# Running sums and outer sums of an attention stage: from VectorE additions to accumulating transfers issued by GpSimd

## The chip, the cores and the metric

The kernel runs on one core of a Trainium2 chip. The metric is the device time of one execution in microseconds; the value compared is the median of three runs. All data are 32-bit floats. In this text TensorE is PE in the profile, VectorE is DVE, ScalarE is ACT, GpSimd is POOL, and SyncE (which only issues transfers) is SP.

## What is computed

Two layers follow each other on an input of shape (2, 512, 64, 64): two images of 4096 pixels with 512 channels. The first is a deformable convolution. The change touches only the second, which is self-attention over the pixels of each image, followed by a linear map and a normalization:

```python
px = jnp.transpose(x.reshape(B, C, N), (0, 2, 1))
q = jnp.tanh(px @ Wq.T)
k = jnp.tanh(px @ Wk.T)
v = px @ Wv.T
scores = jnp.einsum('bip,bjp,p->bij', q, k, align_w)
attn = jax.nn.softmax(scores, axis=2)
content = px + attn @ v
content = content @ Wfc.T + bfc
```

The softmax is computed without a maximum: exponentials of the scores are multiplied with the values, their sum over the keys is formed beside it, and the product is scaled by the reciprocal of that sum at the end.

## The kernel before

The span has three parts: the first layer (up to about 1216 us), and then for each of the two images a projection stage (keys, queries, values) and an attention stage, and at the end the normalization of the whole output.

In the attention stage the 4096 queries of an image are worked off in four **chunks** of 1024 queries, two halves (qh 0 and 1) of 512. The product of values and exponentials is done with a scheme of seven block products in place of eight (a Strassen-like one), and that twice, nested. At the outer level a chunk has seven passes p, each with one block combination of exponentials and one of values (`ORDER`); at the inner level `products` (L1467) does seven matmul groups of 128x128 by 128x256. A pass runs over eight groups of 512 keys (NG = 8) and a ninth that brings the residual in. Pass times group gives 63 **slots** to a chunk (`SLOTS`); slot l does pass l // 9, group l % 9.

For every key group there are four tiles of exponentials, each 128 x 1024: e0 and e1 (first half of the keys of the group, first and second half of the queries), e2 and e3 (second half of the keys). `produce` (L1389) makes one: two matmuls of scores into the single PSUM bank "st", then an exponential on ScalarE. `settle` (L1417) works on it one slot later. `EVENTS` (L1541) is the hand-written table that says in which slot l of its chunk each is made; negative slots lie in the last slots of the chunk before. The combinations for the outer level are formed in place ("outer sums", four of a group):

- `second_row` (L1410): e0 becomes e1 - e0, and e1 becomes e1 + e3 (L1413)
- `at`, L1588: e3 becomes e0 + e3, from slot 30 on, when the fourth pass is done with e3
- `at`, L1590: e2 becomes e2 - e3, from slot 40 on

`transform` (L1385) subtracts one quarter block from another in place, for the inner level. `inner_sums` (L1454) makes three more blocks (tile tt) from an exponential tile, four slots (LEAD) ahead of the products that use them.

The sums over the keys: `add_total` (L1403) adds a tile to the running total of its query half, 128 x 1024; e0 and e2 go to the total of half 0, e1 + e3 to that of half 1. `total` (L1426) adds the two halves of a total's columns; `spread_total` (L1432) sums over the partitions by a matmul with ones (tile pr) and copies the result to rin, which is used to scale the residual (`scale_residual`) and the outputs (`finish`).

All this is under a manual schedule: each engine runs its instructions in the order in which `slot` (L1592) writes them. The big tiles of the stage come from one pool, `ring`, 36 buffers of 4 KB a partition; a tile takes a buffer whose earlier tile has had its last use. The values of a slot (tile v, 448 KB) are loaded by SyncE three slots ahead, into four buffers. `load_queries` fetches the queries of the next chunk into a single buffer q. For the first chunk of an image the events with negative slots are done during the projection stage (`early_scores`, L1674), which leaves the rest of them to its end. GpSimd's only work in these stages is `sum_pixels` in the projections.

Of the kernel before, what the change touches and what calls it, by code (L numbers as in the profile page):

```python
# [10 lines left out]
F32 = mybir.dt.float32  # L11
I32 = mybir.dt.int32
AF = mybir.ActivationFunctionType
ALU = mybir.AluOpType
# [4 lines left out]
P = 128  # L19
# [508 lines left out]
NG = S // P // 4  # L528
# [6 lines left out]
def kernel(ctx: ExitStack, tc: tile.TileContext, t_in: dict, out: bass.AP):  # L535
# [7 lines left out]
    nc.vector.tensor_reduce(al[:, 1:2], al[:, 0:1], AX.X, ALU.max, apply_absolute_value=True)  # L543
    nc.vector.memset(al[:, 0:1], 1.0 / SCORE_MAX)
    window_path(tc, t_in, out, far, sums)


# [27 lines left out]
def window_path(ctx: ExitStack, tc: tile.TileContext, t_in: dict, out: bass.AP, far: bass.AP, sums: bass.AP):  # L575
    nc = tc.nc
# [66 lines left out]
    with ExitStack() as l0:  # L643
# [517 lines left out]
        with tc.manual_schedule():  # L1161
# [60 lines left out]
            for i in range(NSEQ):  # L1222
# [6 lines left out]
                w, m, g = Chain(weights, i + 1), Chain(sample, i), Chain(features, i + 3)  # L1229
# [12 lines left out]
    with ExitStack() as l1, tc.manual_schedule():  # L1242
        HC = C // 2
        HQ = CH // 2
        ring = l1.enter_context(tc.tile_pool(name="w1ring", bufs=36, reuse_waits="tile"))
        bnp = l1.enter_context(tc.tile_pool(name="w1bnp", bufs=1))
        bst = bnp.tile([P, KB, NB * NCH, 6], F32, name="bst")
        bfc = load("L1_conv_bfc", [P, KB], None, bnp)
# [3 lines left out]
        def piece(name, shape=(P, 2, CH)):  # L1252
            return ring.tile(list(shape), F32, tag="r", name=name)
# [15 lines left out]
        with ExitStack() as inner:  # L1269
            wk = inner.enter_context(tc.tile_pool(name="w1work", bufs=1))  # L1270
# [94 lines left out]
            def load_queries(n, k):  # L1365
                q = wk.tile([P, 2, CH], F32, name="q")
                for h in range(2):
                    nc.sync.dma_start(q[h * DQ : (h + 1) * DQ], q_d[n][k])
                return q
# [12 lines left out]
            def blocks(t):  # L1382
                return t.rearrange("p a (s q) -> p (a s) q", s=2)

            def transform(t):  # L1385
                x = blocks(t)
                nc.vector.tensor_sub(x[:, 1], x[:, 1], x[:, 0])
# [14 lines left out]

            def add_total(c, qh, t):  # L1403
                if qh in c.tot:
                    nc.vector.tensor_add(c.tot[qh], c.tot[qh], t)  # L1405
                else:
                    c.tot[qh] = piece("tot")
                    nc.vector.tensor_copy(c.tot[qh], t)

            def second_row(c, g):  # L1410
                t0, t1 = c.e["e0", g], c.e["e1", g]
                nc.vector.tensor_sub(t0, t1, t0)  # L1412
                nc.vector.tensor_add(t1, t1, c.e["e3", g])  # L1413
                if g < NG:
                    add_total(c, 1, t1)

            def settle(c, key, g):  # L1417

                e = c.e[key, g]
                if key in ("e0", "e2"):  # L1420
                    add_total(c, 0, e)
                transform(e)
                if key == "e1":
                    second_row(c, g)

            def total(c, qh):  # L1426
                t = c.tot[qh]
                nc.vector.tensor_add(t[:, 1, :], t[:, 1, :], t[:, 0, :])
                if qh:
                    nc.vector.tensor_add(t[:, 1, HQ:], t[:, 1, HQ:], t[:, 0, :HQ])  # L1430

            def spread_total(c, qh):  # L1432
                p = pair_bank("pr")[:, 0, :]
                nc.tensor.matmul(p, ones, c.tot.pop(qh)[:, 1, :], start=True, stop=True)
                nc.scalar.copy(rin[:, qh, :], p)

            def load_residual(c, qh):
                x = load_chunk(c.n, 2 * c.k + qh, nc.sync, "xq")
                for h in range(2):
                    c.e[f"e{2 * h + qh}", NG] = x[h]  # L1440

            def norm_residual(c, qh):
                for h in range(2):
                    normalize(c.e[f"e{2 * h + qh}", NG], 2 * h, *norms[c.n])

            def scale_residual(c, qh):
                for h in range(2):
                    t = c.e[f"e{2 * h + qh}", NG]
                    nc.vector.tensor_mul(t, t, rin[:, qh, :].unsqueeze(1).to_broadcast([P, 2, CH]))
                    transform(t)  # L1450
                if qh:
                    second_row(c, NG)
# [14 lines left out]
            def products(c, p, g, v, t):  # L1467
                if g == 0:
                    c.acc = bank("accx"), bank("accy")
                ax, ay = c.acc  # L1470
                x = blocks(c.e[ORDER[p][0], g])
                for out, blk, op, first, final in (
                    (ax[:, 0], 0, x[:, 0], True, False), (ax[:, 1], 2, x[:, 2], False, True),
                    (ax[:, 2], 4, t[:, 0], True, True),
                    (ay[:, 0], 3, t[:, 2], True, False), (ay[:, 1], 1, x[:, 1], False, True),
                    (ay[:, 2], 5, x[:, 3], True, False), (ay[:, 3], 6, t[:, 1], False, True),
                ):
                    nc.tensor.matmul(out, v[:, blk, :], op, start=(first and g == 0), stop=(final and g == NG))  # L1478

            def first_copy(c):  # L1480
                ax, ay = c.acc
                u = wk.tile([P, HQ], F32, name="u", bufs=2)
                nc.scalar.copy(u, ax[:, 0])  # L1483
                return u

# [53 lines left out]
                    yield from finish(c, t, 1, 0)  # L1539

            EVENTS = {}  # L1541
            for g, l in enumerate((-14, -13, -11, -10, -9, -7, -6, -5)):
                EVENTS.setdefault(l, []).append(("e0", g))
            for g in range(NG):
                EVENTS.setdefault(g - 4, []).append(("e2", g))
                EVENTS.setdefault(5 + g, []).append(("e3", g))
                EVENTS.setdefault(13 + g, []).append(("e1", g))

            class Attention:

# [5 lines left out]
                def before(self, l, c):  # L1556

                    for done in self.open:
                        settle(*done)
                    self.open = []  # L1560
                    for key, g in EVENTS.get(l, ()):
                        produce(c, key, g)
                        self.open.append((c, key, g))
# [10 lines left out]
                def at(self, l, c, s):  # L1574

                    if l in (-7, 8):
                        load_residual(c, int(l > 0))
                    if l in (-3, 11):
                        norm_residual(c, int(l > 0))
                    if l in (5, 22):  # L1580
                        spread_total(c, int(l > 5))
                        scale_residual(c, int(l > 5))
                    if l in (7, 25):
                        nc.vector.reciprocal(rin[:, int(l > 7), :], rin[:, int(l > 7), :])
                    if l in (6, 24):
                        self.sums(s + 2)
                    if 30 <= l < 31 + NG:
                        nc.vector.tensor_add(c.e["e3", l - 30], c.e["e0", l - 30], c.e["e3", l - 30])  # L1588
                    if 40 <= l < 41 + NG:
                        nc.vector.tensor_sub(c.e["e2", l - 40], c.e["e2", l - 40], c.e["e3", l - 40])  # L1590

                def slot(self, s):  # L1592
                    k, l = divmod(s, SLOTS)
                    c = self.chunks[k]
                    nxt = self.chunks[k + 1] if k + 1 < NCH // 2 else None
                    self.fetch(s + 3)
                    if l % (NG + 1) == 0 and self.ends:
                        next(self.ends[-1], None)
                    self.before(l, c)
                    if nxt and l >= 44:  # L1600
                        if l == 44:
                            nxt.q = load_queries(self.n, k + 1)
                        self.before(l - SLOTS, nxt)
                        self.at(l - SLOTS, nxt, s)
                    self.at(l, c, s)
                    if l + LEAD not in (8, 26):
                        self.sums(s + LEAD)
                    if l in (4, 21):
                        total(c, int(l > 4))
                    p, g = divmod(l, NG + 1)  # L1610
                    products(c, p, g, self.v.pop(s), self.t.pop(s))
                    for e in self.ends[:-1] if g == 0 else self.ends:
                        next(e, None)
                    if g == NG:
                        self.ends = self.ends[-1:] + [collect(c, p, first_copy(c), c.acc)]
# [50 lines left out]
            for n in range(NB):  # L1666
# [1 line left out]
                first = at.chunks[0]  # L1668
                pending = []
                early_events = deque(  # L1670
                    (l, key, g) for l in range(-16, 0) for key, g in EVENTS.get(l, ())
                )

                def early_scores():  # L1674
# [76 lines left out]
                for done in at.open:  # L1751
                    settle(*done)
# [5 lines left out]
                for s in range(NCH // 2 * SLOTS):  # L1758
                    at.slot(s)
                    l = s - (NCH // 2 - 1) * SLOTS  # L1760
# [88 lines left out]
```

## Time and profile before

| what | us |
|---|---|
| median of three runs (lowest to highest) | 3673.21 (3672.21 to 3676.82) |
| the profiled execution | 3674.86 |
| its span, first to last instruction | 3673.1 |
| TensorE busy | 3239.0 |
| VectorE busy | 2969.6 |
| ScalarE busy | 1362.9 |
| GpSimd busy | 272.5 |

The page divides the span into 40 slices and gives the busy share of each engine in tenths, the TensorE clock that was granted, and the busy share of the DMA engines. The attention stages are roughly slices 16 to 26 and 29 to 38, counted from 0:

```profile
PE   5789999999998867899899898998889989899890
DVE  8899999999995577877887878778787787877864
DMA  6334334334232454344353443555434344344379
```

What the reader sees: TensorE is nearly full in the attention stages, VectorE three quarters full, the DMA engines under half. An average over a stage doesn't tell which engine is waited for; that is read from the waits and the timeline.

### The profile page before, as it was taken

How to read it: one execution, taken by the hardware profiler on the slowest of the kernel's cores; microseconds unless marked ns; L12 is line 12 of the kernel's file. 1: busy time of each engine (PE TensorE's matmuls, PEld its weight loads, DVE VectorE, ACT ScalarE, POOL GpSimd, SP SyncE). 2: the span in 40 equal slices, each digit the busy share in tenths (PEclk: the TensorE clock that was granted, in tenths of full speed). 3: DMA queues.
4: the chain of work that ended last, by engine and by line, in shares of the span. 5: the costliest groups of instructions: out<-in, count | busy, mean ns of one | idle time of the engine just before them, and what ended most of it. 6: DMA issues, size and time to landing. Idle time of an engine off the chain costs nothing.

```text
span 3673.1 us, 37956 instructions
## 1 busy us (share of the span) xinstructions
PE 3239.0 (88%) x14147; PEld 2261.1 (62%) x14147; DVE 2969.6 (81%) x4107; ACT 1362.9 (37%) x1802; POOL 272.5 (7%) x186
## 2 busy tenths in 40 slices
PE   5789999999998867899899898998889989899890
PEld 2355555555555645686676776876577676686670
DVE  8899999999995577877887878778787787877864
ACT  2577778778775312203112022022202202203105
POOL 1121121121120110000000000011000000000000
PEclk9889999999999978999999999999899999999995
DMA  6334334334232454344353443555434344344379
GB/s 211 97 116 139 120 100 127 109 108 131 94 105 102 163 198 160 117 147 151 116 160 123 135 151 108 185 175 202 156 121 154 123 142 139 113 151 146 113 299 349
DMA packets 201634, 537.67 MB, mean 146 GB/s; under 512 B 25024, under 2 KB 26816, under 8 KB 200416
## 3 DMA queue, kind: packets, MB, share of 16 engines
q1 hardware_dynamic: 193920, 514.18, 41.9%
q10 hardware_dynamic: 7488, 20.97, 1.7%
q8 instruction: 113, 1.85, 0.2%
q14 instruction: 81, 0.66, 0.1%
q0 software_dynamic: 32, 0.00, 0.0%
HBM read 410.15 MB, written 124.91 MB: 146 GB/s over the span
## 4 chain that ended last, share of the span: by engine, by line
PE 63%; DVE 27%; DMA 4%; ACT 3%; issue 1%; POOL 1%; SPq 0%; ACTq 0%; DVEq 0%; POOLq 0%
PE accy L1478 20%; PE accx L1478 16%; DVE conv L820 9%; PE py L1004 6%; PE pS L1396 5%; PE pq L789 5%; PE pa L984 5%; DVE tot L1405 2%; DVE e L1412 2%; DVE e L1413 2%; PE pvy L1633 2%; PE pk L1700 1%; DVE tt L1458 1%; DVE vform L1332 1%; PE pvx L1633 1%
## 5 line engine op out<-in xcount | busy, mean ns | idle before, releaser
L1478 PE MATMUL accy<-tt,v 128*128 128x256 f32 x2016 | 602.2, 380 | 0.0
L1400 ACT ACTIVATE e<-pS 128x1024 f32<-128x1024 f32 x256 | 261.8, 1023 | 895.0 <-PE pS L1396 785.6
L1478 PE MATMUL accx<-e,v 128*128 128x256 f32 x1792 | 489.1, 396 | 25.8 <-DMA v<-wv 15.3
L1478 PEld LDWEIGHTS accx<-e,v 128*128 128x128 f32 x1792 | 329.5, 193 | 226.4 <-issue 153.1
L1478 PE MATMUL accy<-e,v 128*128 128x256 f32 x1792 | 461.7, 380 | 0.0
L820 DVE SCALAR_TENSOR_TENSOR conv<-xn,L_conv_dw_w_sb,conv 128x504 f32<-128x504 f32 (+1 forms) x512 | 409.4, 808 | 36.6 <-ACT conv L814 22.7
L1478 PEld LDWEIGHTS accy<-tt,v 128*128 128x128 f32 x2016 | 385.0, 191 | 53.0
L1478 PEld LDWEIGHTS accy<-e,v 128*128 128x128 f32 x1792 | 342.5, 191 | 47.3
L1396 PE MATMUL pS<-q,keys 64*128 64x512 f32 x1024 | 294.7, 653 | 35.1 <-ACT e L1400 25.5
L1458 DVE TENSOR_TENSOR tt<-tt,e 128x512 f32<-128x512 f32 x448 | 310.0, 692 | 15.3
L1478 PE MATMUL accx<-tt,v 128*128 128x256 f32 x1008 | 302.8, 382 | 0.0
L1457 DVE TENSOR_TENSOR tt<-e 128x256 f32<-128x256 f32 x448 | 187.6, 419 | 140.9 <-PE accy L1478 139.8
L984 PEld LDWEIGHTS pa<-bt,patch 96*128 96x128 f32 x2048 | 249.6, 196 | 57.1 <-issue 35.1
L984 PE MATMUL pa<-bt,patch 96*128 96x128 f32 x2048 | 253.1, 280 | 7.0 <-ACT bt L970 5.6
L970 ACT COPY bt<-pb 96x1024 f32<-96x1024 f32 x124 | 234.8, 2009 | 57.8 <-PE pb L965 53.9
L1483 ACT COPY u<-accx 128x256 f32<-128x256 f32 x56 | 20.9, 373 | 619.5 <-PE accx L1478 619.5
L789 PE MATMUL pq<-in_w,xn 128*128 128x512 f32 x512 | 239.3, 611 | 7.1 <-DVE o L882 5.0
L1004 PE MATMUL py<-dT,L_conv_out_w_sb 128*128 128x512 f32 x512 | 237.6, 609 | 4.7 <-ACT dT L995 4.7
L1405 DVE TENSOR_TENSOR tot<-tot,e 128x1024 f32<-128x1024 f32 x176 | 214.9, 1221 | 29.1 <-ACT e L1400 27.1
L1478 PEld LDWEIGHTS accx<-tt,v 128*128 128x128 f32 x1008 | 193.8, 192 | 27.1
L877 PE MATMUL po<-om_w_pg,feat 128*128 128x432 f32 x512 | 202.9, 540 | 3.0 <-ACT feat L860 3.0
L995 ACT COPY dT<-pa 32x256 f32<-32x256 f32 x496 | 179.6, 362 | 66.3 <-PE pa L984 57.0
(215 smaller groups left out, 4316.2 us busy)
## 6 DMA issues: line engine op xcount, KB each, us to landing
v<-wv SPq DMA_DIRECT2D x448, 448.0 KB
wv<-vform SPq DMA_DIRECT2D x112, 448.0 KB
patch<-xt SPq DMA_DIRECT2D x256, 192.0 KB
v<-ww SPq DMA_DIRECT2D x56, 448.0 KB
xt<-xj SPq DMA_DIRECT2D x128, 128.0 KB
res<-in_x SPq DMA_DIRECT2D x64, 256.0 KB
wx<-res SPq DMA_DIRECT2D x64, 256.0 KB
xq<-wx SPq DMA_DIRECT2D x32, 512.0 KB
```

The lines of the kernel that those rows point to most:

```text
L789: nc.tensor.matmul(pq, xn[:, kb, 1 + 2 * t : 3 + 2 * t, :].rearrange("p r c -> p (r c)"), in_w[:, kb, :], start=(kb == 0), stop=(kb == KB ...
L820: nc.vector.scalar_tensor_tensor(dst, src, wt, dst, ALU.mult, ALU.add)
L877: nc.tensor.matmul(po[:, : 3 * GP], f[:, kb, t * P : (t + 1) * P], om_w[:, kb].rearrange("p a k g -> p (a k g)"), start=(kb == 0), stop=(k ...
L970: copy(bt[:SN].rearrange("s g q d -> s d (g q)")[:, d0 : d0 + 4, :], pb[:SN])
L984: nc.tensor.matmul(pa[:, p], xp[:SN, p, cb * P : (cb + 1) * P], bt[:SN, 4 * cb : 4 * cb + 4, PX * s + p, :], start=True, stop=True,)
L1004: nc.tensor.matmul(py, out_w[:, kb, cb * P : (cb + 1) * P], dT[:, kb, :], start=(kb == 0), stop=(kb == KB - 1))
L1396: nc.tensor.matmul(p[:, a, :], keys[r, i, (2 * u + h) * P : (2 * u + h + 1) * P], c.q[r, qh, :], start=True, stop=True)
L1400: nc.scalar.activation(e.rearrange("p a q -> p (a q)"), p.rearrange("p a q -> p (a q)"), AF.Exp)
L1405: nc.vector.tensor_add(c.tot[qh], c.tot[qh], t)
L1457: nc.vector.tensor_sub(t[:, 0], x[:, 1], x[:, 3])
L1458: nc.vector.tensor_add(t[:, 1:3], t[:, 0].unsqueeze(1).to_broadcast([P, 2, HQ]), x[:, 0:3:2])
L1478: nc.tensor.matmul(out, v[:, blk, :], op, start=(first and g == 0), stop=(final and g == NG))
```

## The change

`add_total`, the addition of e3 in `second_row` and the addition at L1588 are no longer VectorE instructions but transfers from one SBUF tile to another that add to their destination, issued by GpSimd; the ninth group of `second_row` (the residual) stays on VectorE. The first tile of a total is still copied by VectorE. In `settle` the transform now stands ahead of the addition to the total, so what is added to total 0 is the transformed tile, and `total` undoes this for both halves with one more addition. Events are moved: e0 to slots -18 to -11, e2 to -9 to -2, e3 to 0 to 7 and e1 to 9 to 18 with two gaps (before: -14 to -5, -4 to 3, 5 to 12, 13 to 20). `total` of half 1 moves from slot 21 to 22, its `spread_total` from 22 to 23, the sum at L1588 from 30 to 29, the load of the next queries from slot 44 to 43. The ring has 38 buffers, u one in place of two.

```diff
@@ -1242,7 +1242,7 @@
     with ExitStack() as l1, tc.manual_schedule():
         HC = C // 2
         HQ = CH // 2
-        ring = l1.enter_context(tc.tile_pool(name="w1ring", bufs=36, reuse_waits="tile"))
+        ring = l1.enter_context(tc.tile_pool(name="w1ring", bufs=38, reuse_waits="tile"))
         bnp = l1.enter_context(tc.tile_pool(name="w1bnp", bufs=1))
         bst = bnp.tile([P, KB, NB * NCH, 6], F32, name="bst")
         bfc = load("L1_conv_bfc", [P, KB], None, bnp)
@@ -1402,7 +1402,7 @@
 
             def add_total(c, qh, t):
                 if qh in c.tot:
-                    nc.vector.tensor_add(c.tot[qh], c.tot[qh], t)
+                    nc.gpsimd.dma_start(c.tot[qh], t, accum_op=ALU.add)
                 else:
                     c.tot[qh] = piece("tot")
                     nc.vector.tensor_copy(c.tot[qh], t)
@@ -1410,24 +1410,25 @@
             def second_row(c, g):
                 t0, t1 = c.e["e0", g], c.e["e1", g]
                 nc.vector.tensor_sub(t0, t1, t0)
-                nc.vector.tensor_add(t1, t1, c.e["e3", g])
                 if g < NG:
+                    nc.gpsimd.dma_start(t1, c.e["e3", g], accum_op=ALU.add)
                     add_total(c, 1, t1)
+                else:
+                    nc.vector.tensor_add(t1, t1, c.e["e3", g])
 
             def settle(c, key, g):
 
                 e = c.e[key, g]
+                transform(e)
                 if key in ("e0", "e2"):
                     add_total(c, 0, e)
-                transform(e)
                 if key == "e1":
                     second_row(c, g)
 
             def total(c, qh):
                 t = c.tot[qh]
                 nc.vector.tensor_add(t[:, 1, :], t[:, 1, :], t[:, 0, :])
-                if qh:
-                    nc.vector.tensor_add(t[:, 1, HQ:], t[:, 1, HQ:], t[:, 0, :HQ])
+                nc.vector.tensor_add(t[:, 1, HQ:], t[:, 1, HQ:], t[:, 0, :HQ])
 
             def spread_total(c, qh):
                 p = pair_bank("pr")[:, 0, :]
@@ -1479,7 +1480,7 @@
 
             def first_copy(c):
                 ax, ay = c.acc
-                u = wk.tile([P, HQ], F32, name="u", bufs=2)
+                u = wk.tile([P, HQ], F32, name="u")
                 nc.scalar.copy(u, ax[:, 0])
                 return u
 
@@ -1539,12 +1540,11 @@
                     yield from finish(c, t, 1, 0)
 
             EVENTS = {}
-            for g, l in enumerate((-14, -13, -11, -10, -9, -7, -6, -5)):
-                EVENTS.setdefault(l, []).append(("e0", g))
-            for g in range(NG):
-                EVENTS.setdefault(g - 4, []).append(("e2", g))
-                EVENTS.setdefault(5 + g, []).append(("e3", g))
-                EVENTS.setdefault(13 + g, []).append(("e1", g))
+            for g, l in enumerate((9, 10, 12, 13, 14, 16, 17, 18)):
+                EVENTS.setdefault(g - 18, []).append(("e0", g))
+                EVENTS.setdefault(g - 9, []).append(("e2", g))
+                EVENTS.setdefault(g, []).append(("e3", g))
+                EVENTS.setdefault(l, []).append(("e1", g))
 
             class Attention:
 
@@ -1577,15 +1577,15 @@
                         load_residual(c, int(l > 0))
                     if l in (-3, 11):
                         norm_residual(c, int(l > 0))
-                    if l in (5, 22):
+                    if l in (5, 23):
                         spread_total(c, int(l > 5))
                         scale_residual(c, int(l > 5))
                     if l in (7, 25):
                         nc.vector.reciprocal(rin[:, int(l > 7), :], rin[:, int(l > 7), :])
                     if l in (6, 24):
                         self.sums(s + 2)
-                    if 30 <= l < 31 + NG:
-                        nc.vector.tensor_add(c.e["e3", l - 30], c.e["e0", l - 30], c.e["e3", l - 30])
+                    if 29 <= l < 30 + NG:
+                        nc.gpsimd.dma_start(c.e["e3", l - 29], c.e["e0", l - 29], accum_op=ALU.add)
                     if 40 <= l < 41 + NG:
                         nc.vector.tensor_sub(c.e["e2", l - 40], c.e["e2", l - 40], c.e["e3", l - 40])
 
@@ -1597,15 +1597,15 @@
                     if l % (NG + 1) == 0 and self.ends:
                         next(self.ends[-1], None)
                     self.before(l, c)
-                    if nxt and l >= 44:
-                        if l == 44:
+                    if nxt and l >= 43:
+                        if l == 43:
                             nxt.q = load_queries(self.n, k + 1)
                         self.before(l - SLOTS, nxt)
                         self.at(l - SLOTS, nxt, s)
                     self.at(l, c, s)
                     if l + LEAD not in (8, 26):
                         self.sums(s + LEAD)
-                    if l in (4, 21):
+                    if l in (4, 22):
                         total(c, int(l > 4))
                     p, g = divmod(l, NG + 1)
                     products(c, p, g, self.v.pop(s), self.t.pop(s))
@@ -1668,7 +1668,7 @@
                 first = at.chunks[0]
                 pending = []
                 early_events = deque(
-                    (l, key, g) for l in range(-16, 0) for key, g in EVENTS.get(l, ())
+                    (l, key, g) for l in range(-18, 0) for key, g in EVENTS.get(l, ())
                 )
 
                 def early_scores():
```

## The prediction

> **What bounds the kernel now.** I read the table of windows first, over one chunk of the attention stage (63 slots; some 247 us from the pr sum of one chunk to that of the next), then the waits of TensorE, then the rows of the VectorE instructions that the change touches, then the timeline of the slots in which TensorE stands still. Columns of the windows: busy time (count) of each engine, granted clock, DMA share, GB/s.
>
> ```profile
> 1953.00:2041.00 88.00, 75.10 (x311) 50.47 (x310) 69.25 (x95) 21.85 (x25) 0.00 (x0) 0.95 0.37 121
> 2041.00:2200.00 159.00, 159.00 (x705) 125.47 (x704) 129.99 (x184) 25.41 (x32) 0.00 (x0) 1.00 0.46 145
> ```
>
> In the second part of the chunk TensorE is busy all the time; in the first it is idle for 12.9 us of 88. So a chunk can give at most about 13 us, eight of them 103 us, whatever is taken off VectorE. The waits of TensorE over the whole run say where:
>
> ```profile
> PE pr L1434 <- DVE tot L1430: 82.5, 8, 10.3
> PE pS L1396 <- ACT e L1400: 25.5, 28, 1.2
> PE accx L1478 <- DMA v<-wv: 15.3, 5, 13.1
> PE accx L1478 <- DVE tt L1457: 10.5, 1, 10.5
> ```
>
> Eight waits of 10.3 us, one a chunk: the sum over keys of the second query half (pr) waits for its running total. The timeline shows why VectorE is late there:
>
> ```profile
> 2033.43 1.23 DVE L1412 TENSOR_TENSOR e<-e 128x1024 f32<-128x1024 f32 x1
> 2034.69 1.23 DVE L1413 TENSOR_TENSOR e<-e 128x1024 f32<-128x1024 f32 x1
> 2035.95 1.23 DVE L1405 TENSOR_TENSOR tot<-tot,e 128x1024 f32<-128x1024 f32 x1
> ...
> 2038.15 0.69 DVE L1428 TENSOR_TENSOR tot<-tot 128x512 f32<-128x512 f32 x1
> 2038.87 0.42 DVE L1430 TENSOR_TENSOR tot<-tot 128x256 f32<-128x256 f32 x1
> ...
> 2039.44 2.05 PE L1434 MATMUL pr<-tot,ones_k 128*128 128x512 f32 x2 [10.32 <-DVE tot L1430]
> ```
>
> In the eight slots that make e1, VectorE does 0.42+0.69 (inner sums) +0.42 (transform) +3x1.23 = 5.2 us where TensorE needs 4.28 us (3.02 in a slot without scores):
>
> ```profile
> 1982.71 1.13 PE L1478 MATMUL accx<-e,v 128*128 128x256 f32 x4
> ...
> 1986.99 1.13 PE L1478 MATMUL accx<-e,v 128*128 128x256 f32 x4
> ```
>
> It falls behind by 0.9 us a slot and by what else comes (collecting, scaling), until pr waits.
>
> ```profile
> L1405 DVE TENSOR_TENSOR tot<-tot,e 128x1024 f32<-128x1024 f32 x176 | 214.9, 1221 | 29.1 <-ACT e L1400 27.1
> L1413 DVE TENSOR_TENSOR e<-e 128x1024 f32<-128x1024 f32 x64 | 78.4, 1225 | 2.2
> L1588 DVE TENSOR_TENSOR e<-e 128x1024 f32<-128x1024 f32 x64 | 77.9, 1218 | 0.0
> al_f<-in_L_conv_align_w POOLq DMA_DIRECT2D x1, 0.2 KB, 6.9
> ```
>
> The last line is the only transfer that GpSimd issues before: 6.9 us to landing at the kernel's start, 0.66 us on GpSimd by its row. No accumulating transfer is in this trace.
>
> **What the Trainium skill says.** "DMA: Bandwidth & Descriptors", section on the anatomy of a GpSimd-issued DMA, fits 2.0 us plus bytes at 436 GB/s and says most of the 2 us is the write receipt, heaviest for HBM; no run here shows it. The same page, in its rules, says an accumulating DMA reads its destination and writes it later, so a second one on the same bytes has to wait for the first's semaphore: each addition to one total is a full round trip. "Collectives: The Full Stack", section on the bandwidth ceiling, says the add needs two source reads and so halves the rate. Nothing here confirms either.
>
> **The change part by part.** Removed from VectorE: 176 total adds x 1.22, 64 L1413 adds x 1.225, 64+8 L1588 adds x 1.22: 215+78+88 = 381 us; added 8 x 0.42 in total(). VectorE is not the bound outside the e1 slots, so this is worth only the stalls above. An e1 slot costs VectorE 2.8 us after it, under 4.28.
>
> Added: 312 transfers of 512 KB, 39 a chunk. Price of one, D: with one read counted 0.66+2.0+1.2 = 3.9 us, with two 0.66+2.0+2.4 = 5.1 us. I take 4.5: source and destination are both SBUF, where the receipt should be short, but loads share the engines.
>
> First total (e0, e2): 15 additions in a chain, first score in slot -18, total needed in slot 4, sum in slot 5. From the second event to there lie about 17 slots of 4.28 and three of 3.02, some 82 us, plus a little lead: 15 x 4.5 = 68 fits, 15 x 5.1 = 77 fits, from about 5.8 us on it is late. This is why the scores' four slots count.
>
> Second total: for each e1, transfer A adds e3 to it, transfer B adds it to the total, and B must wait for A. GpSimd is in order, so the next group's A is queued behind B's wait; nothing but such transfers is behind it there. The cycle c is A's trip with B's bytes in front of it on the same queue: 5.1 us at one read (0.66+2.0+2x1.2), 7.5 at two; I take 6.0. Slots after the change: scores in 9, 10, 12, 13, 14, 16, 17, 18, without one in 11 and 15 (3.02 us). From the start of slot 9, A can start (2.4 us for score and exponential, 0.42 and 1.23 on VectorE) at 4.1, 8.4, 15.7, 20.0, 24.3, 31.6, 35.8, 40.1. With D 4.5 and c 6.0 the ends of A from the third on are 20.2, 26.2, 32.2, 38.2, 44.2, 50.2; the last B ends at 54.7, total() adds 1.15: 55.9. pr now stands in slot 23, which starts at 52.4 (8x4.28+2x3.02 to slot 19, four of 3.02). Wait 3.5 us where it was 10.3: -6.8 x 8 = -54 us. The inner sums of the last e1 need A's end at 50.2 and TensorE its slot 25 at 58.4: covered.
>
> Waits of scores for the exponential in the same slots (two of 0.7 us a chunk, from buffers VectorE frees late) go: -1.5 x 8 = -12. Next late is the residual: spread one slot later leaves VectorE three slots, not four, for two multiplications, two transforms and two row sums (about 9 us with the copy of rin, against 9.1+1.8): I charge 1 us a chunk, +8.
>
> e3 += e0 (slots 29 to 37): one independent transfer every 3.02 us with three slots to the inner sums and four more to TensorE; hidden at D below some 15 us, if the engines keep up. The first addition of the second total is a copy on VectorE that waits for A (4.5 us); inner sums run four slots ahead, so it is covered.
>
> Queries are loaded in slot 43 and first used in 45, not 44 and 49: 6 us for 256 KB on SP behind one load of v. Hidden; if not, 1 to 3 us a chunk. Two more ring buffers and one less u: the e1 of group 7 is now made before an e1 is freed, so the two buffers keep the exponential from waiting; one u is free nine slots before its next use. Nothing.
>
> First chunk of each image: four more scores (2.25 us each, one bank) at the end of the projections. They fall into a gap (TensorE waits 13.1 us for the first v) and leave four slots 1.26 us shorter; but the last forms on VectorE, which that v waits for, come later in the queue. VectorE also drops 11 adds there (13 us). I set nothing, within 10 us either way an image.
>
> Sum against the profiled execution (3674.86 us, 1.8 around its span): -54-12+8 = -58, 3617. It lies 1.65 above the median of 3673.21: 3615.
>
> **The rivals.** One read, D 3.9, c 5.1: last B at 49.6, total at 50.7, no wait: -82-12+8 = -86, 3587. For: TensorE at 100% wherever VectorE is not late. Against: loads already take 37 to 46% of the DMA engines.
>
> Two reads with everything serial, D 5.1, c 7.5: A ends at 20.8, then 28.3 ... 58.3, B 63.4, total 64.5, wait 12.1, so +14-12+8 = +10: 3683 or, with a few us in the first chunks, no change.
>
> The DMA engines become the bound (slower). 145 GB/s at share 0.46 means some 315 GB/s for all sixteen; 39 x 0.52 MB x 2 reads in 247 us is 165 GB/s more, share 0.98. Then D grows past 5.8 and the first total's chain is late at slot 5: at 6.5, 15 x 0.7 = 10 us; c 8 makes pr wait 17.4 instead of 10.3, 7 us: +17 x 8 -12+8 = +132, 3805; at 6.0, some 3 and 3 us, 3717. It decides from D 5.8 on. For: the share; against: it counts the time packets took, and 348 GB/s were moved at 0.92 in the last stage.
>
> That VectorE isn't relieved can't be: the order of instructions has 312 adds fewer on it.
>
> **How the numbers follow.** Forecast 0.34; no wait at pr 0.23; two reads, serial 0.12; engines bound 0.31. The serial case is the one near zero: 0.07 within 0.2% (7 us, about what a measurement of this kernel can tell), the rest of it slower. Faster 0.57, same 0.07, slower 0.36. Likeliest case's own range: 3595 to 3650. Whole range: 3565 (no wait, and the first chunks gain 10 each) to 3790 (engines at D 6.4), leaving 0.05 below and 0.14 above.
>
> **What would show it.** Right: pr's wait on the total at 2 to 6 us, eight times; DVE near 2590 us; DMA share in the chunk's first half 0.6 to 0.8; accumulating transfers landing in 4 to 5 us. Wrong: a wait of TensorE or VectorE on tot in slot 4 or 5 (first total late), transfers landing in 6 us or more, new waits for v or q, or PE idle in the 3.02 us slots.

## The result, and the profile after

| | us |
|---|---|
| before, median of three | 3673.21 |
| after, median of three (lowest to highest) | 3921.08 (3919.97 to 3932.52) |
| after, profiled execution and its span | 3932.52, 3930.7 |

The ratio of after to before is 1.0682, 95% interval 1.0649 to 1.0714: slower by 6.8%. The change did what it says: VectorE's busy time fell from 2969.6 to 2607.7 us. TensorE waits more all the same. Its waits over the whole run after the change (engine, line, what it waited for: us in total, times, longest):

```profile
PE pr L1435 <- DVE tot L1431: 282.8, 16, 26.1
PE accx L1479 <- DMA v<-wv: 30.3, 36, 8.4
PE pS L1396 <- ACT e L1400: 22.7, 20, 1.2
PE accy L1479 <- DVE ct L1509: 18.1, 15, 3.6
```

Before, pr waited eight times, for the second total of each chunk. Now it waits sixteen times, for both totals of each chunk, and over three times as long in sum, +200 us: 87 us for the eight first totals (7.3 to 16.1 each) and 196 us for the eight second ones (21.5 to 26.1 each). The other rows add 15 us (v late) and 18 us (a PSUM bank not yet emptied, see below). VectorE isn't the cause but stands in between, as its own waits between 1500 and 2600 us show:

```profile
DVE tt L1458 <- DMA e<-e: 123.4, 23, 8.6
DVE tot L1430 <- DMA tot<-e: 58.0, 7, 19.1
DVE tot L1408 <- DMA e<-e: 22.9, 4, 6.4
```

L1430 is total(), L1458 the inner sums: VectorE, which is done early, waits for transfers to land. The issues of the transfers (KB each, median us from issue to landing) and the busy time by stretch of one chunk (second row: from the first pr sum to the second; third: after it):

```profile
tot<-e POOLq DMA_DIRECT2D x176, 512.0 KB, 5.3
e<-e POOLq DMA_DIRECT2D x128, 512.0 KB, 8.2
```

```profile
1940.00:2044.00 104.00, 90.54 (x378) 61.30 (x377) 47.91 (x83) 28.20 (x33) 12.89 (x15) 0.93 0.78 199
2044.00:2142.00 98.00, 71.45 (x297) 52.24 (x296) 49.55 (x76) 16.01 (x20) 13.05 (x15) 0.85 0.73 181
2142.00:2187.00 45.00, 43.68 (x201) 38.08 (x200) 31.63 (x48) 0.74 (x2) 7.74 (x9) 0.99 0.76 200
```

VectorE is half idle (49.55 of 98), TensorE is idle for 26.6 us of the same stretch, and the DMA engines went from shares of 0.37 to 0.46 to 0.73 to 0.78. GpSimd's own timeline in that chunk shows the two rhythms. First the chain of the first total, then the pairs of the e1 slots (L1414 is the outer sum, L1405 the addition to the total):

```profile
1997.63 0.86 POOL L1405 DMA_DIRECT2D tot<-e  x1 [6.31 <-DMA tot<-e]
2003.98 0.86 POOL L1405 DMA_DIRECT2D tot<-e  x1 [5.49 <-DVE tt L1459]
2009.82 0.86 POOL L1405 DMA_DIRECT2D tot<-e  x1 [4.98 <-DMA tot<-e]
...
2035.92 0.86 POOL L1405 DMA_DIRECT2D tot<-e  x1 [4.04 <-DMA tot<-e]
...
2088.66 0.86 POOL L1405 DMA_DIRECT2D tot<-e  x1 [7.74 <-DVE tt L1458]
2089.19 1.21 POOL L1414 DMA_DIRECT2D e<-e  x1
2097.62 0.86 POOL L1405 DMA_DIRECT2D tot<-e  x1 [7.21 <-DMA e<-e]
2098.15 1.21 POOL L1414 DMA_DIRECT2D e<-e  x1
2106.73 0.86 POOL L1405 DMA_DIRECT2D tot<-e  x1 [7.37 <-DVE tt L1458]
```

The six links from 1997.63 to 2035.92 take 6.4 us each, where a score comes every 4.28; pairs come every 9.0 us, where the slots give 5.04. (The mean link of a whole chunk is 6.3 to 6.9 us, the first chunk of each image apart. Where the bracket names VectorE in the pairs, VectorE had itself been released by the landing that the pair waited for; at 2003.98 its instruction only ended at about the same time.) Both totals are late for that reason.

A stall also costs after its end. TensorE's timeline around one (start, duration, matmuls):

```profile
2041.64 2.05 PE L1435 MATMUL pr<-tot,ones_k 128*128 128x512 f32 x2 [13.46 <-DVE tot L1431]
2043.47 1.91 PE L1479 MATMUL accx<-e,v 128*128 128x256 f32 x4
2045.18 1.06 PE L1479 MATMUL accx<-tt,v 128*128 128x256 f32 x2
2046.04 1.06 PE L1479 MATMUL accy<-tt,v 128*128 128x256 f32 x2
...
2049.50 1.13 PE L1479 MATMUL accx<-e,v 128*128 128x256 f32 x4
2050.47 0.59 PE L1479 MATMUL accx<-tt,v 128*128 128x256 f32 x2
```

The same groups take 1.91 and 1.06 us right after the stall and 1.13 and 0.59 us a slot later. TensorE's busy time grew from 3239.0 to 3285.9 us with the same 14147 matmuls. So +191 (pr, both kinds of wait on it: 282.8 against 82.5 + 9.0), +15 (v), +18 (PSUM), -10 (one wait for tt, gone) and +47 (slower matmuls) make 261; the spans differ by 258. The 47 us aren't all behind these stalls: part of them may lie in slots that wait for v, as the run with the sum of the fourth pass alone shows below.

### The profile page after: what moved, and what is told of

The parts are those of the page before. It is cut to its first block, busy times and chain, and to the rows that moved or that the text cites. A ratio compares the mean times of both kernels' runs of the same rounds, so it can differ in the third digit from the quotient of the medians.

```text
span 3930.7 us, 38681 instructions
## 1 busy us (share of the span) xinstructions
PE 3285.9 (84%) x14147; PEld 2277.6 (58%) x14147; DVE 2607.7 (66%) x3803; ACT 1363.1 (35%) x1802; POOL 542.3 (14%) x498
## 3 DMA queue, kind: packets, MB, share of 16 engines
q0 software_dynamic: 44960, 163.60, 22.1%
## 5 line engine op out<-in xcount | busy, mean ns | idle before, releaser
L1458 DVE TENSOR_TENSOR tt<-e 128x256 f32<-128x256 f32 x448 | 188.1, 420 | 555.6 <-PE accy L1479 300.9
L1479 PE MATMUL accx<-e,v 128*128 128x256 f32 x1792 | 502.2, 404 | 30.4 <-DMA v<-wv 30.3
L1405 POOL DMA_DIRECT2D tot<-e x176 | 151.4, 860 | 1315.3 <-DVE e L1387 409.0
L1396 PE MATMUL pS<-q,keys 64*128 64x512 f32 x1024 | 305.3, 668 | 31.6 <-ACT e L1400 22.7
L1459 DVE TENSOR_TENSOR tt<-tt,e 128x512 f32<-128x512 f32 x448 | 309.9, 692 | 15.3
L1435 PE MATMUL pr<-tot,ones_k 128*128 128x512 f32 x32 | 32.7, 1127 | 282.8 <-DVE tot L1431 282.8
```

Of the source, the lines that this page charges most:

```text
L1396: nc.tensor.matmul(p[:, a, :], keys[r, i, (2 * u + h) * P : (2 * u + h + 1) * P], c.q[r, qh, :], start=True, stop=True)
L1405: nc.gpsimd.dma_start(c.tot[qh], t, accum_op=ALU.add)
L1458: nc.vector.tensor_sub(t[:, 0], x[:, 1], x[:, 3])
L1459: nc.vector.tensor_add(t[:, 1:3], t[:, 0].unsqueeze(1).to_broadcast([P, 2, HQ]), x[:, 0:3:2])
```

## The experiments

Two theories. **Theory 1**: a transfer is a round trip, the additions to one total are a chain of them, and in the e1 slots GpSimd's order makes one cycle out of two. **Theory 2**: the bytes of loads and additions together fill the DMA engines. Each kernel below is the changed one with the edit shown; the last four start from the first one, the schedule alone. Diffs are cut to the lines that matter. Without an interval, the time is that of a single execution or two; before was at 3673.2 to 3676.9 us in these sessions.

**The schedule alone.** All additions go back to VectorE; the new slots stay.

```diff
-                    nc.gpsimd.dma_start(c.tot[qh], t, accum_op=ALU.add)
+                    nc.vector.tensor_add(c.tot[qh], c.tot[qh], t)
-                    nc.gpsimd.dma_start(t1, c.e["e3", g], accum_op=ALU.add)
+                    nc.vector.tensor_add(t1, t1, c.e["e3", g])
-                        nc.gpsimd.dma_start(c.e["e3", l - 29], c.e["e0", l - 29], accum_op=ALU.add)
+                        nc.vector.tensor_add(c.e["e3", l - 29], c.e["e0", l - 29], c.e["e3", l - 29])
```

> The changed kernel with all 312 additions back on VectorE: only the moved scores, the ring and the order inside settle are left of the change. Theory 1 (the accumulating transfers are the whole loss; the new slots are harmless or good, as e1 slots now last 5.04 us on average against 5.5 us of VectorE work): no wait for a first total, the wait of pr for the second total well under 10 us a chunk, 3590 to 3660 us. Rival (the moved scores or the buffers cost something themselves, in the first chunks above all): 3690 us or more.

Measured: 3608.88 us, ratio to before 0.9815 (0.9798 to 0.9831). TensorE's waits and one chunk up to the second pr sum and after it:

```profile
PE pr L1435 <- DVE tot L1431: 23.6, 8, 3.0
PE accx L1479 <- DMA v<-wv: 16.7, 6, 7.2
```

```profile
1926.00:2014.00 88.00, 83.92 (x362) 60.72 (x360) 73.69 (x103) 21.16 (x25) 0.00 (x0) 1.00 0.43 135
2014.00:2173.00 159.00, 158.57 (x688) 120.84 (x689) 130.03 (x186) 29.17 (x36) 0.00 (x0) 0.99 0.46 142
```

So the change is two things of opposite sign: moved scores (with the larger ring, the single u and the order in `settle`, which were not tried apart), which alone take 1.85% off, and the transfers, which add 312 us to that. VectorE does the same work as before; it's spread over ten slots in place of eight ahead of a sum that comes one slot later.

**Only the totals by transfers** (the last two of the three edits above).

> Only the running totals by transfers (22 a chunk), all outer sums on VectorE. Theory 1 (serial round trips of 6.1 us a link): the wait of pr for the first total stays at some 14 us a chunk; the second total's chain, no longer behind transfers of another kind, takes 6.1 a link in place of 9.2, so its wait falls from some 20 to 3 to 8 us; 3750 to 3820 us. Theory 2 (traffic: loads and additions together fill the DMA engines): with 44% of the added bytes gone, landing falls from 5.3 to under 4.7 us and the first total's wait goes mostly; under 3720 us.

Measured: 3729.0 us. The totals landed in 5.4 us, not less than with all transfers, so removing 44% of the bytes (the queue moved 92.29 MB in place of 163.60) didn't shorten them. pr's waits:

```profile
PE pr L1435 <- DVE tot L1431: 129.8, 16, 17.0
```

Of these, 102 us are for the first totals (7.3 to 17.0 each), whose wait stays as theory 1 has it, and 28 us for the second ones (2.0 to 7.4). Theory 1, in a time a little under its range.

**Only the two outer sums by transfers**, totals on VectorE one event later.

```diff
-                    nc.gpsimd.dma_start(c.tot[qh], t, accum_op=ALU.add)
+                    nc.vector.tensor_add(c.tot[qh], c.tot[qh], t)
-                    add_total(c, 1, t1)
+                    if g:
+                        add_total(c, 1, c.e["e1", g - 1])
+                    if g == NG - 1:
+                        add_total(c, 1, t1)
```

> Only the two outer sums by transfers (17 a chunk), totals on VectorE, each e1 added to its total one event later so that VectorE does not stand at the transfer. Theory 1: the transfers are independent of each other and land in about 5.3 us; no total waits for a chain; 3580 to 3650 us. Theory 2: transfers of outer sums still land in 7 us or more and v is still late; 3680 us or more.

Measured: 3678.87 us, just under what theory 2 expected and outside what theory 1 did. The outer sums of the e1 slots landed in 6.3 us, longer than an event even without totals on the queue, so VectorE stood at them and pr waited 58.9 us; v was late 35 times. Theory 1 as I had stated it, with transfers that cost nothing once they don't depend on each other, is wrong here.

**The total's addition behind the next outer sum** in GpSimd's order (the lower half of the edit above, with transfers).

> The changed kernel, with the addition of an e1 to its total issued behind the next group's outer sum, so that GpSimd no longer stands at it. Theory 1 (GpSimd's queue makes one cycle out of two round trips): the cycle falls from 9.2 to about 6 to 6.5 us, the second total's wait from some 20 us to 3 to 8 us, the first total's stays; 3790 to 3840 us. Theory 2 (bytes): cycle stays near 9, no change from 3921 us.

Measured: 3862.28 us. Outer sums were issued at 2067.95, 2075.88, 2083.24 and 2090.50 us, every 7.5 us in place of 9.0 (over all chunks the additions to the second total follow each other every 7.9 us, where it was 9.0). GpSimd's order is part of the cycle, but a smaller one than expected; 59 us of the loss go with it.

**Two thirds of the value loads left out.**

```diff
-                        self.v[s] = load_values(self.n, *divmod(s % SLOTS, NG + 1))
+                        p, g = divmod(s % SLOTS, NG + 1)
+                        self.v[s] = self.v[s - 1] if g % 3 else load_values(self.n, p, g)
```

(and `products` takes `self.v[s]` without removing it)

> The changed kernel, but the values are loaded only for every third slot and used in three slots (so two thirds of the products use the values of another key group): the loads beside the additions fall from 448 KB to 149 KB a slot. Theory 1 (an addition's round trip is its own: fixed part plus its own bytes): totals still land in 5.0 to 5.3 us, outer sums of the e1 slots in 7 us or more, the waits of pr stay near 280 us; 3880 us or more. Theory 2 (loads and additions share full DMA engines): totals land in about 4.4 us, the shortest seen beside the loads, the first total's wait nearly goes; under 3780 us.

Measured: 3816.28 us, between the two. Issues and landing:

```profile
tot<-e POOLq DMA_DIRECT2D x176, 512.0 KB, 4.5
e<-e POOLq DMA_DIRECT2D x128, 512.0 KB, 6.3
```

Totals land in 4.5 us, where theory 2 put them: the loads are 0.8 us of the 5.3. An undisturbed link now takes 4.9 to 5.1 us (issues at 1941.26, 1946.15, 1951.12), and the mean link of a chunk 5.5 to 5.7, the first chunk of each image apart. In those chunks the first wait of pr falls to 1.1 to 5.3 us, where it was 7.3 to 13.5; so it more than halves, but it isn't gone. In the first chunk of an image it stays near 14 us. The pairs still take 7.9 us on average, and the second waits fall only from 196 to 163 us in sum, nearer to theory 1. Each theory holds in part: loads beside the additions make them land later. That the DMA engines are full, as theory 2 says, holds only in places of the changed kernel: their share was 0.76 to 0.87 while the first total's chain ran (1940 to 2040 us), 0.74 to 0.98 in the pairs and 0.91 to 1.06 in the slots of the fourth pass. What the single links of 7 to 10 us wait for, which stand in every chain, with few loads too, was not looked at and stays open.

**Half of each transfer left out.**

```diff
-                    nc.gpsimd.dma_start(c.tot[qh], t, accum_op=ALU.add)
+                    nc.gpsimd.dma_start(c.tot[qh][:, 0, :], t[:, 0, :], accum_op=ALU.add)
```

(and so for the other two)

> The changed kernel with each accumulating transfer cut to the first 512 of its 1024 columns, 256 KB (the other half of each sum is left out). Tells the fixed part from the part that goes with the bytes. Theory 1a (mostly a fixed round trip): totals land in 4.5 us or more, cycle of the e1 transfers 7.5 us or more, 3800 us or more. Theory 1b (mostly bytes, two reads and a write): totals land in under 4 us, cycle near 6 us, no wait for the first total, 3600 to 3680 us.

**Copies in place of additions** (`accum_op` dropped).

> The changed kernel with the same transfers, waits and order, but copying in place of adding (each sum is replaced by its last addend). Theory 1b (the second read of an addition costs as much as the first): totals land in about 3.8 us, outer sums of the e1 slots in 5, no wait for the first total, 3600 to 3680 us. Theory 1a (a fixed round trip): totals land in 4.8 us or more, waits stay, 3850 us or more.

Measured: 3667.24 and 3653.64 us. The landings of the totals, shortest, median and longest, in the changed kernel, with half the bytes, and as copies:

```profile
DMA to landing us min/median/max: 4.4/5.3/10.2
```

```profile
DMA to landing us min/median/max: 3.2/3.8/9.9
```

```profile
DMA to landing us min/median/max: 2.8/3.7/8.6
```

Half the bytes take 1.2 us off the shortest and 1.5 off the median; so some 2.0 us are fixed and 2.4 go with 512 KB when nothing is in the way. A copy of the same bytes is 1.6 us shorter, and all the copies' packets took 11.3% of 16 engines' span where those of the additions took 22.1%. That fits an addition paying for a second read of its destination; the runs show the doubled time and not the read itself. Either cut removes the first total's wait (0.3 us of one is left with copies); pairs come every 6.6 and 6.5 us on average, and pr waits 72 and 67 us in all. Most of the cost goes with the bytes.

**Two first totals**, for even and odd groups, added at the end by VectorE.

```diff
-                    add_total(c, 0, e)
+                    add_total(c, (0, "odd")[g % 2], e)
```

> The changed kernel with two running totals for the first query half, for even and odd key groups, added by VectorE at the end: the chain of 15 dependent transfers becomes two of 7. GpSimd still issues in the same order, but each waits for the one before the last. Theory 1 (the dependent chain makes the first total late): no wait of pr for the first total (some 14 us a chunk before), the second total's stays near 20; 3780 to 3830 us. Theory 2 (bytes): the transfers land later in proportion as they overlap, the wait stays; 3880 us or more.

Measured: 3844.91 us. The first total's wait is gone in every chunk, which only the chain explains, since the transfers landed later (6.2 us), not sooner. The second total's eight waits are as long as before (193.9 us, where they were 195.6 with one first total), and v was late for 41.7 us in place of 30.3. The 76 us that were saved are about what the first total's waits had been (87 us).

**Fewer transfers in the good schedule.** Three kernels start from the schedule alone. The first has only the outer sums of e1 by transfers and adds each e1 to its total two events later:

```diff
-                    add_total(c, 1, t1)
+                    c.m.setdefault("late", []).append(t1)
+                    if len(c.m["late"]) > 2:
+                        add_total(c, 1, c.m["late"].pop(0))
```

(`total` adds what is left in the list)

> The new slots with only the e1 outer sums by transfers (8 a chunk, independent of each other); totals and the sum at the fourth pass on VectorE, each e1 added to its total two events later and the last two just ahead of total(). Theory (a transfer helps where nothing depends on it for two slots and none queues behind another): landing about 6 us, never waited for by a total; VectorE drops 1.2 us in each e1 slot, the remaining 3.0 us of pr go; 3580 to 3605 us, below the 3609 of the schedule alone. Rival (inner sums of e1 wait for landings, v comes later): 3610 us or more.

Measured: 3623.36 us, ratio 0.9862 (0.9846 to 0.9879): slower than the schedule alone. Landing 6.4 us; pr waited 34.1 us in place of 23.6. In the chunk looked at, the two additions that were put off stand right ahead of the total (2.47 us), and VectorE waits 0.38 and 1.44 us for landings in the inner sums before them, as the rival has it; the runs don't part the two.

The second has only the sum of the fourth pass (L1588) by transfers:

> The new slots with only the sum e3 + e0 of the fourth pass by transfers (9 a chunk). The prediction priced it at nothing: landing 6 to 10 us is covered by seven slots. If right: 3600 to 3612 us, as the schedule alone (3609). Rival (it makes the loads of v late, as waits for v rose from 15 to 30 us in the changed kernel): 3620 us or more, with waits for v in the 3.02 us slots.

Measured: 3635.88 us (two executions), 27 above the schedule alone, though nothing waits for these sums. The bytes have a price through v, which was late for 16.7 us in 6 waits with the schedule alone:

```profile
PE accx L1479 <- DMA v<-wv: 29.1, 35, 8.2
PE pr L1435 <- DVE tot L1431: 23.6, 8, 3.0
```

The waits themselves are only 12.4 us of it; TensorE's busy time grew by 15.3 us as well. The slots just behind these transfers wait some 0.4 us for v and take 3.6 to 3.7 us in all, where a slot without scores takes 3.02. While the transfers run the DMA engines' share is 0.99 (1802 to 1829 us), where it is some 0.5 in these slots of the schedule alone: here they are full.

The third gives the second total's additions to GpSimd's arithmetic (`nc.gpsimd.tensor_add` for half 1):

> The new slots, no transfers; the additions to the second total are done by GpSimd's own arithmetic (56 additions of 128 x 1024, some 2.4 us each by the row of its pixel sums), all else on VectorE. If GpSimd and VectorE don't hinder each other: VectorE drops 1.2 us in each e1 slot, GpSimd needs 2.4 of 5.0 us, pr doesn't wait; 3575 to 3600 us. Rival (the two share a way into SBUF, and VectorE's two-input additions stretch): VectorE's rows in these slots well above 1.22 us, 3610 us or more.

Measured: 3658.33 us, ratio 0.996 (0.9945 to 0.9974); pr waited 52.1 us. The timeline of an e1 slot shows the rival:

```profile
1997.82 2.37 POOL L1405 TENSOR_TENSOR tot<-tot,e 128x1024 f32<-128x1024 f32 x1 [2.97 <-DVE e L1414]
1998.03 2.72 DVE L1459 TENSOR_TENSOR tt<-tt,e 128x512 f32<-128x512 f32 x1
...
2007.06 0.69 DVE L1459 TENSOR_TENSOR tt<-tt,e 128x512 f32<-128x512 f32 x1
```

The VectorE addition that starts just after a GpSimd addition takes 2.72 us in place of 0.69 and ends 0.56 us after it, about its own usual length; the instructions after it have their usual length. That fits a VectorE instruction that is held and then runs, and not one that is slowed: the Trainium skill says so in "SBUF — State Buffer", section on who interferes with whom (a VectorE instruction with two SBUF inputs and a GpSimd instruction that reads SBUF contend for a port pair that one of them holds alone). VectorE saves 1.2 us and loses 2.0 by each.

**Later differences.** For the last three groups e1 - e0 is formed in slots 24 to 26:

```diff
+                    if l in (24, 25, 26):
+                        t0, t1 = c.e["e0", l - 19], c.e["e1", l - 19]
+                        nc.vector.tensor_add(t0, t0, c.e["e3", l - 19])
+                        nc.vector.tensor_sub(t0, t1, t0)
```

(and `second_row` leaves their difference out)

> The new slots, all on VectorE; for the last three groups the difference e1 - e0 is not formed in the e1 slots but in slots 24 to 26, from the sums there already are (two VectorE instructions in place of one, 1.22 us each, no further buffer). If the loss left in the schedule alone is VectorE's lateness in the e1 slots (pr waits 3.0 us a chunk, 3.7 us are moved behind it): pr's wait goes to under 0.5 us a chunk, -24 us and some restart time, 3575 to 3595 us. Rival (the two more instructions in the 3.02 us slots make VectorE late there): 3605 us or more.

Measured: 3661.99 us, ratio 0.9966 (0.9954 to 0.9978). pr's wait for the total is gone, and a new one stands in its place:

```profile
PE accy L1480 <- DVE ct L1510: 74.3, 8, 9.3
```

The six instructions stand ahead of the collection of the third pass, which has to empty a PSUM bank before the fourth can go on. With them stand inner sums and a reciprocal of 3.35 us, which are there in the schedule alone too. Of all these kernels the schedule alone is the fastest.

## Why the prediction was wrong

The forecast was 3615 us, its range ended at 3790, and the time is 3921.

- **The bound before** was read rightly: VectorE late in the e1 slots, 13 us a chunk to gain, no more. The schedule alone took pr's eight waits from 10.3 to 3.0 us each.
- **The price of one transfer, D, is the step that failed.** I took 4.5 us, under the 5.1 that two reads gave, and put no figure on the loads of v that share the engines with it. At the shortest, an addition of 512 KB lands in 4.4 us, the 2.0 us plus two reads at 436 GB/s of the Trainium skill ("DMA: Bandwidth & Descriptors", the anatomy of a GpSimd-issued DMA, with the second read of "Collectives: The Full Stack", the bandwidth ceiling): that estimate was good to 0.1 us. (A landing is counted from the start of the issue: the last addition shown was issued at 2035.92, and VectorE went on at 2040.38.) From a landing to the next issue go some 0.5 us more, for which I had no term; by its size the 0.66 that I charged for the issue stands in for it, and an undisturbed link with few loads was 4.9 to 5.1. Beside the loads the link is 6.4, and the mean link of a chunk went from 5.6 to 6.5 by them. So the 5.1 of two reads was near the price without loads, and the loads put 0.8 to 0.9 us on top. My reason for going under (a short receipt in SBUF) is not borne out by the runs.
- **The cycle c** was sized at 6.0, at most 7.5; it is 9.0. With few loads it is 7.9, near the two-read end; the loads are the rest.
- **The arithmetic on top of D and c held.** With D 6.4 its chain is 15 x 0.6 = 9 us late (measured 13.5 in the chunk shown, whose mean link was 6.8). With c 9.0 the third A ends near 22, the last near 67, the total near 75: a wait of 22 us at slot 23 (measured 25.9 there). (One sum is off, without effect: with one read the last B ends at 49.0 and not at 49.6.) The rival that I priced at 3805 with D 6.5 and c 8 is the one that came true in its result, both totals late; its premise, engines at a share of 0.98, holds in some slots only, and not where the first total's chain ran (0.76 to 0.87). Its point of decision, D 5.8, lies between the links of 4.9 to 5.1 us, where the first total was nearly in time, and 6.4.
- **That slow case was itself priced too low**: c was still too small, TensorE's slower matmuls, most visibly after stalls, were left out (47 us), and so were the waits of v and of the PSUM bank (33 us).
- **The sum of the fourth pass at nothing** was wrong: 27 us, by late v and busier TensorE slots, at full DMA engines. I had asked when its result is needed, and not what its bytes push aside.
- **"Inner sums run four slots ahead, so it is covered"** was wrong for VectorE in the changed kernel. In the e1 slots it stands at a landing with its later work queued behind, collections among it: that is 12.6 of the 18 us of accy. The other 5.5 us come after the second total, and the schedule alone has them too (6.0).
- **The scores' waits**, taken as -12, fell by 2.8. Their two waits a chunk went, 11.7 us in all, but the four more scores at the end of each image's projections brought 8.9 us back, which I had set at nothing.
- **The moved scores** were not priced by themselves. They were the only gain in the change. That the schedule alone takes 3609 us, close to my 3615, doesn't bear out the forecast, which put its gain down to the transfers.

That relieving VectorE would be worth only its stalls, that DMA share would rise to 0.6 to 0.8, and that VectorE would end near 2590 us (2607.7) was right.

## What to carry to other kernels

When work goes from an engine to the DMA engines, price a dependent chain by its link, from issue to the next issue, beside the loads that run there already, and compare that with the interval at which its inputs come. Ask of each added byte what transfer it delays, even where nothing waits for its own result. And when a change moves a schedule and an engine at once, run the schedule alone: here it was the better kernel.

## What the runs showed of the hardware

- An accumulating transfer issued by GpSimd from SBUF to SBUF landed at the shortest in 4.4 us for 512 KB and 3.2 us for 256 KB; a plain copy of 512 KB in 2.8 us.
- With two thirds of the loads of v left out, the additions to the totals landed in 4.5 us (median), beside all of them in 5.3; the mean link of a chain went from 5.6 to 6.5 us, the first chunk of an image apart.
- GpSimd took 0.86 us to issue an addition (1.75 us for two in a row, from 2079.17 to 2080.92), 0.53 us for a copy.
- After a stall of 13.5 us TensorE's matmuls took nearly twice as long for some 5 us. The length of that stretch did not follow the stall's: after 25.9 us (at 2139.26) it was some 3.5 us.
- A GpSimd addition of 128 x 1024 (2.37 us) held one VectorE addition from 0.69 to 2.72 us.
